# Heads of a score unit in three spare PSUM banks, held work released at once, and loads one stage ahead, in a planned transformer block

## The chip, the cores and the metric

The kernel runs on one core of a Trainium2 chip. The metric is device time in microseconds (us), the median of several executions of the whole program. A program starts its five engines side by side; each works through its own instructions in order, and they meet at semaphores. PE is TensorE (matmuls; PEld its weight loads), DVE is VectorE, ACT is ScalarE, POOL is GpSimd, and SP here only issues DMAs, also in order.

## The reference

One transformer block with adaptive layer norm, in fp32: 8 sequences of 1024 tokens, width 512, 16 heads of 32, an MLP of width 2048.

```python
mod = silu(condition) @ Wada + bada
sh_a, sc_a, gt_a, sh_m, sc_m, gt_m = split(mod, 6, axis=1)
xm = layernorm(x, g1, be1) * (1 + sc_a) + sh_a
x = x + gt_a * attention(xm, Wqkv, Wproj, bproj)   # causal, softmax over keys
xm = layernorm(x, g2, be2) * (1 + sc_m) + sh_m
h = gelu(xm @ W1 + b1, approximate=False)
x = x + gt_m * (h @ W2 + b2)
```

`x` and the output are (8, 1024, 512), `condition` is (8, 512).

## The kernel before

**Blocks and two streams.** The kernel treats 16 blocks n = 0..15, two halves of 512 tokens for each of 8 sequences; `h` is 0 for a first half, 1 for a second. Two streams share PE. The *attention stream* (`attend`, L1392) goes over the blocks and in each over 4 groups of 4 heads. The *linear stream* (`linear`, L1069) is a generator that goes through a list of steps by window, `plan[w]` (L228 to L264): `k`, `q`, `v` projections, `at` and `mt` (transposes of the normalized input for attention and for the MLP), `proj` (output projection, L844), `u` (four up projections, L865), `d` (four parts of the down projection, L914), and the loads and gate rows that they need. While attention works on block n, the linear stream does the output projection and MLP of block n-1 and the projections of later blocks. The last window, `plan[NB]`, has no attention beside it.

**The planner.** Nothing of the order is decided on the chip. While the program is written, the kernel keeps its own estimate of when each engine is free (`now`) and when each buffer is written or read for the last time (`written`, `left`; L104 `due`). A value that is not yet even issued has the time `NEVER`, infinity. The linear stream yields what its next matmul needs; `wait_of` (L1092) makes a waiting time of it, and `linear_wait` (L1103) is the smallest over the main linear thread and its side threads (transposes, and the last two products of a Strassen projection, run as side threads). Before each piece of attention, `step_aside` (L1135) fills PE with linear matmuls as long as the attention piece would wait longer than the linear one, or as long as the linear stream is behind its pace (`stream["due"]`, raised by `pace`). If `linear_wait` is `NEVER`, the loop breaks at once and attention is issued, wait or no wait.

**Attention by units.** A *score unit* (`scores`, L1196) makes scores of 128 queries by up to 512 keys for the 4 heads of a group into the PSUM tile `sc`, 4 banks (L1208); DVE adds the causal mask on diagonal units (L1220) and takes the row maxima (L1228). A *weight unit* (`weights_T`, L1282) makes the transposed scores `st` in the same 4 banks (L1294, maxima subtracted by L1305), ACT exponentiates them into `pT` (L1317), POOL zeroes what lies above the diagonal (L1322) and adds the units of a group for the row sums (L1429). `weigh` (L1334) multiplies with v into `po` (L1345). `finish` (L1355) sums over partitions (L1363), ACT copies, DVE inverts in four pieces (L1378), POOL multiplies (L1383); after the fourth group of a block this sets `attended`, for which `proj` of that block waits. The PSUM tile `st`/`sc` has one buffer: the next unit's matmuls wait until DVE or ACT has read it. Three further banks (`banks`, L163) belong to the linear stream and to the small sums of `finish` and `maxima_rows` (L1260). The eighth bank is `po`.

The score units of a group are issued during the group ahead of it. In `attend` each weight unit is a slot k of n_slots, and `upto` (L1406 to L1408) says how many score units of the next group are to be issued by the end of that slot. A block with h = 0 has 3 weight and 3 score units a group, one with h = 1 has 7 of each.

**Held work.** DVE work that can wait (statistics, inversions) is put in `jobs` and issued when DVE is not ahead of PE in the plan (L500). ACT work that changes the function table (the square root of a layer norm, `root` L551; the normalization `apply` L558; `gelu` L868) is put in `excursions`; `run_excursions(1)` issues one after each weight unit (L1417) and, in blocks with h = 0, one after each score unit (L1436). `work` (L1106) issues everything held when the linear stream has nothing to do, but `step_aside` does not call it then.

**Preparation.** The Strassen sums of the weights W1 and W2 are made once, in 8 stages of 4 sums (`preparation`, L670): four loads by SP, 12 us of planned waiting, four sums by `either` (L148: DVE or POOL, whichever is free by its rule), each stored to DRAM by SP. It advances only when POOL or DVE is not ahead of PE in the plan (L694). The first up projection issues all that is left before it goes on (L883).

**Weights.** `fetch` (L321) loads weight pieces through a ring of 9 buffers on SP, in the order in which the plan will use them (`order`, L310).

Of the kernel before, what the change touches and what calls it, by code (L numbers as in the profile page):

```python
# [22 lines left out]
def kernel(  # L23
# [33 lines left out]
    nc = tc.nc  # L57
# [167 lines left out]
    def mlp_steps(n):  # L225
# [7 lines left out]
        + [("mod", 3), ("at", 2), ("v", 1), ("mod", 4), ("k", 2), ("gates", "m"), ("columns_m",)],  # L233
    }
    late = []
    for w in range(1, NB):
        n = w - 1
        m = mlp_steps(n)
        even = blocks[n][1] == 0
        rows_a = [("rows", blocks[n][0], "a")] if even else []  # L240
        rows_m = [("rows", blocks[n][0], "m")] if even else []
        own = m[:1] + ([("load_xa", w + 2)] if w + 2 < NB else []) + m[1:3]
        own += [("norm_a", w + 2)] if w + 2 < NB else []
        if w == NB - 1:
            steps = late + [("load_xr", n)] + rows_a + [("proj", n), ("v", w)]
            steps += [("mt", n)] + rows_m + own + m[3:6]
            late = m[6:]
        else:

            steps = late + [("v", w), ("load_xr", n)] + rows_a + [("proj", n), ("k", w + 1)]  # L250
            if w == 1:
                steps = [("load_xr", n)] + rows_a + [("proj", n)]
            steps += [("mt", n), ("q", w + 1)] + rows_m + own
            at = [("at", w + 2)] if w + 2 < NB else []
            if blocks[w][1] == 0:

                steps += m[3:5]
                late = m[5:6] + at + m[6:]
            else:
                steps += m[3:6] + at  # L260
                late = m[6:]
        plan[w] = steps
    n = NB - 1
    plan[NB] = [("load_xr", n), late[0], ("proj", n), late[1], ("mt", n)] + mlp_steps(n)  # L264
# [21 lines left out]
    def pieces_of(step):  # L286
# [4 lines left out]
        if kind == "gates":  # L291
            return [(Wada, GATES[step[1]][0], kh, fh) for kh, fh in RAW]
        if kind == "proj":
            return [(Wproj, 0, k) for k in range(NC)]
# [224 lines left out]
    def excursion(job, first=False):  # L519
        if alone[0]:  # L520
            job()
        else:
            excursions.insert(0 if first else len(excursions), job)

    def run_excursions(limit=None):
        n = len(excursions) if limit is None else min(limit, len(excursions))
        for _ in range(n):
            excursions.pop(0)()
# [4 lines left out]
    def normalize(tiles, key, sources):  # L533
# [8 lines left out]
        def statistics(t):  # L542
            st = small.tile([P, nc.vector.BN_STATS_DIM], F32, tag="st", name=f"st_{key}_{t}")
            nc.vector.bn_stats(st, tiles[t])
            nc.vector.bn_aggr(mv[:, t, :], st)
            note("DVE", 850, [sources[t]], [("mv", key)])
            if t == NTT - 1:
                excursion(root)
                excursion(apply)
# [120 lines left out]
    def preparation():  # L670

        for w in (W1, W2):
            for i in range(NQ):
                stage = act.tile([P, NC, TB], F32, tag="hT", name=f"prep_{LABEL[id(w)]}_{i}", bufs=NQ)
                got = {}
                for j, kf in enumerate(RAW):
                    a = next(a for a in ("A11", "A12", "A21", "A22") if FULL[a] == kf)
                    got[a] = stage[:, j, :]
                    nc.sync.dma_start(
                        got[a].rearrange("p (k n) -> p k n", n=HB), quarter(w, i, *kf)  # L680
                    )
                ready = now["PE"] + 12000
                for out, a, b, op, name in IN_PLACE:
                    yield ready
                    keys = [("prep", w is W2, i, a), ("prep", w is W2, i, b)]
                    either(got[out], got[a], got[b], op, keys, [("prep", w is W2, i, out)])
                    keep(w, i, name, got[out])
# [3 lines left out]
    def run_preparation(everything=False):  # L691
        while prepared[0] is not None:
# [4 lines left out]
            try:  # L697
                prepared[0][1] = next(prepared[0][0])
            except StopIteration:
                prepared[0] = None  # L700

# [163 lines left out]
    def up(step):  # L865
# [11 lines left out]
        def finished():  # L877
            if q == NQ - 1:
                written["m used", n] = 0.0
            excursion(gelu, first=True)  # L880

        if (n, q) == (0, 0):
            run_preparation(True)  # L883
# [128 lines left out]
    def perform(step):  # L1012
# [28 lines left out]
        elif kind == "at":  # L1041
            n = step[1]
            guards = [("m used", n - 3)] if n > 2 else [("v done", 0)] if n == 2 else []
            start(modulated(f"a{n}", *columns_of["a"], blocks[n][0], guards))
        elif kind == "sums":
# [12 lines left out]
        elif kind == "preps":  # L1058
            prepared[0] = [preparation(), 0.0]
        elif kind == "rows":  # L1060
# [45 lines left out]
    def work():  # L1106

        if linear_wait() == NEVER:
            run_jobs(True)
            run_excursions()  # L1110
        assert linear_wait() < NEVER
# [23 lines left out]
    def step_aside(reads, writes):  # L1135


        while threads():
            own, other = wait_of((reads, writes)), linear_wait()
# [56 lines left out]
    def scores(n, g, parts):  # L1196
# [5 lines left out]
        reads = [("qT", n), ("kT", n - h + parts[0][1])]  # L1202
        step_aside(reads, ["st"])
# [28 lines left out]
        if units[unit_at[0] + 1 :] == [] or units[unit_at[0] + 1][:2] != (n, g):  # L1232
            split_maxima(n, g, h)
# [158 lines left out]
    def attend():  # L1392
        previous = None
        for n in range(NB):
# [5 lines left out]
            for g in range(NC):  # L1400
                nxt = groups.index((n, g)) + 1
                for k in range(n_slots):
                    upto = len(units)
                    if nxt < len(groups):
                        lo, m = first_unit[groups[nxt]], len(score_units(*groups[nxt]))
                        upto = lo + min(m, -(-(k + 2) * m // n_slots))  # L1406
                        if k == n_slots - 1 and nxt + 1 < len(groups):
# [6 lines left out]
            for g, k, upto in slots:  # L1414
# [16 lines left out]
                previous = (n, g, parts, pT, slot, k == n_slots - 1)  # L1431
                while unit_at[0] < upto:
# [4 lines left out]
                    pace(ns)  # L1437
        return previous
# [104 lines left out]
```

## Time and profile before

| what | value |
|---|---|
| median of 3 executions | 3678.65 us (3678.53 to 3679.02) |
| the profiled execution | 3678.31 us, of which the span of instructions is 3676.6 us |
| mean granted TensorE clock | 0.993 |
| DVE busy | 2158.9 us, 59% |
| ACT busy | 1327.8 us, 36% |
| POOL busy | 2044.1 us, 56% |
| DMA | 430.34 MB, a mean of 117 GB/s |
| PE busy in 300 to 400 us / 1000 to 1100 / 2800 to 2900 | 99.63 / 99.99 / 99.99 us of 100 |
| PE busy in 100 to 200 / 200 to 300 / 3300 to 3400 / 3500 to 3600 | 84.04 / 88.87 / 88.83 / 90.70 us of 100 |

The share of PE is an average over stages. In most of the span PE is busy without a break; the four stretches in the last row are where it is not. A stretch is best read by the idle time in front of single PE instructions, which the timeline names with the instruction that ended it. Busy time of PE also grows where the granted clock is lower, with no more work done.

### The profile page before, as it was taken

The page shows a single profiled execution, that of the slowest core. Times are in us where ns is not written, and L with a number is a line of the kernel's source. Part 1 is how long each engine was busy: PE and PEld are TensorE (multiplying, and loading weights), DVE is VectorE, ACT ScalarE, POOL GpSimd, SP SyncE. Part 2 cuts the span into 40 slices and gives each one's busy share as a digit, 9 for nine tenths or more (in the row PEclk, how much of TensorE's full clock was granted, in tenths as well). Part 3 has the DMA queues.
Part 4 walks back from the last instruction along what each step waited for, and adds up shares of the span by engine and source line. Part 5 has one row for each costly group of instructions (what it writes and reads, how often), then busy time and mean ns, then how long its engine had stood idle before and what let it go on. Part 6 is the DMA issues. An engine that isn't in the chain of part 4 may idle for free.

```text
span 3676.6 us, 121132 instructions
## 1 busy us (share of the span) xinstructions
PE 3575.4 (97%) x54821; PEld 1767.9 (48%) x54821; DVE 2158.9 (59%) x2447; ACT 1327.8 (36%) x1412; POOL 2044.1 (56%) x2064
## 2 busy tenths in 40 slices
PE   8889999999999999999999999999999999998989
PEld 4424445445554455544445454444544445454445
DVE  5756675564746557465565666646666465654542
ACT  2334334252333523335242452424425144341421
POOL 3576645656455663566536665356653556444661
PEclk9989999999999999999999999999999999999999
DMA  6633333433333343433434333343333433333334
GB/s 208 195 118 99 119 94 107 126 103 122 112 110 118 105 125 111 139 96 97 125 108 136 97 98 119 113 132 101 102 119 111 134 104 113 105 106 122 89 111 133
DMA packets 307893, 430.34 MB, mean 117 GB/s; under 512 B 25900, under 2 KB 176236, under 8 KB 307380
## 3 DMA queue, kind: packets, MB, share of 16 engines
q1 hardware_dynamic: 307264, 422.56, 38.1%
q8 instruction: 432, 7.08, 0.8%
q14 instruction: 81, 0.66, 0.1%
q10 hardware_dynamic: 116, 0.03, 0.0%
HBM read 394.12 MB, written 28.38 MB: 115 GB/s over the span
## 4 chain that ended last, share of the span: by engine, by line
PE 86%; DVE 7%; ACT 2%; POOL 2%; issue 2%; DMA 0%; SPq 0%; ACTq 0%; POOLq 0%; DVEq 0%
PE bank L199 58%; PE st L1294 8%; PE sc L1208 8%; PE po L1345 7%; DVE mx L1228 2%; PE st L1305 2%; PE bank L1363 2%; POOL pT L1429 1%; PE bank L606 1%; ACT pT L1317 1%; DVE hT L929 1%; DVE sc L1220 1%; DVE xr L156 1%; DVE t_m L156 1%; PE bank L1268 0%
## 5 line engine op out<-in xcount | busy, mean ns | idle before, releaser
L1429 POOL TENSOR_TENSOR pT<-pT,pT 128x512 f32<-128x512 f32 (+3 forms) x1280 | 1207.8, 979 | 548.7 <-ACT pT L1317 382.4
L1317 ACT ACTIVATE pT<-st 128x2048 f32<-128x2048 f32 (+1 forms) x320 | 546.4, 1708 | 1020.1 <-PE st L1305 972.5
L199 PE MATMUL bank<-w,hT 128*32 128x256 f32 x14336 | 808.7, 380 | 4.9 <-DVE hT L929 2.1
L1228 DVE TENSOR_REDUCE mx<-sc 128x4 f32<-128x2048 f32 (+3 forms) x384 | 668.9, 1756 | 205.4 <-PE sc L1208 198.7
L199 PEld LDWEIGHTS bank<-w,hT 128*32 128x32 f32 x14336 | 453.2, 110 | 357.8 <-issue 61.3
L199 PE MATMUL bank<-xm_m,w 128*32 128x256 f32 x8192 | 506.5, 380 | 0.5 <-DVE u_u L191 0.5
L1322 POOL TENSOR_SCALAR_AFFINE_SELECT pT<-pT 128x512 f32<-128x512 f32 x256 | 177.8, 706 | 576.2 <-ACT pT L1317 575.9
L199 PE MATMUL bank<-t_m,w 128*32 128x256 f32 x6144 | 383.1, 380 | 2.4 <-DVE t_m L625 1.0
L1294 PE MATMUL st<-qT,kT 32*128 32x512 f32 (+3 forms) x3072 | 343.0, 531 | 37.1 <-DVE mx L1228 35.8
L199 PEld LDWEIGHTS bank<-xm_m,w 128*32 128x32 f32 x8192 | 254.3, 110 | 248.9 <-issue 95.8
L1208 PE MATMUL sc<-kT,qT 32*128 32x512 f32 (+3 forms) x3072 | 340.2, 527 | 10.5 <-DVE mx L1228 5.8
L1345 PE MATMUL po<-pT,v 128*32 128x512 f32 (+3 forms) x3072 | 315.6, 498 | 6.5 <-POOL pT L1322 6.5
L1220 DVE TENSOR_TENSOR sc<-sc,mask 128x512 f32<-128x512 f32 (+1 forms) x192 | 167.9, 875 | 251.2 <-PE sc L1208 223.0
L199 PEld LDWEIGHTS bank<-t_m,w 128*32 128x32 f32 x6144 | 193.0, 110 | 174.3 <-issue 50.2
L199 PE MATMUL bank<-w,qT 128*32 128x512 f32 x2048 | 243.1, 602 | 6.1 <-POOL qT L1383 3.2
L199 PE MATMUL bank<-xm_a,w 128*32 128x256 f32 x3968 | 243.1, 381 | 0.0
L1378 DVE RECIPROCAL rec<-rec 128x128 f32<-128x128 f32 x256 | 223.6, 917 | 21.0 <-ACT rec L1369 21.0
L1294 PEld LDWEIGHTS st<-qT,kT 32*128 32x128 f32 x3072 | 129.5, 185 | 202.0 <-issue 60.7
L1208 PEld LDWEIGHTS sc<-kT,qT 32*128 32x128 f32 x3072 | 126.8, 184 | 175.0 <-ACT pT L1317 84.7
L191 DVE TENSOR_TENSOR hT<-bank,u_u 128x512 f32<-128x512 f32 x192 | 130.3, 686 | 120.4 <-PE bank L199 118.4
L199 PE MATMUL bank<-t_a,w 128*32 128x256 f32 x2944 | 186.6, 382 | 0.0
L1317 ACT ACT_TABLE_LOAD x88 | 112.9, 1283 | 183.2 <-PE st L1305 182.5
(184 smaller groups left out, 3552.9 us busy)
## 6 DMA issues: line engine op xcount, KB each, us to landing
w<-in_L_cond_W_dram SPq DMA_DIRECT2D x384, 256.0 KB, 2.9
w<-kept_up_S SPq DMA_DIRECT2D x256, 256.0 KB, 2.6
w<-kept_down_S SPq DMA_DIRECT2D x256, 256.0 KB, 2.7
w<-kept_qkv_S SPq DMA_DIRECT2D x180, 256.0 KB, 2.9
w<-in_L_cond_Wqkv_dram SPq DMA_DIRECT2D x147, 256.0 KB, 3.5
hat<-in_x_dram SPq DMA_DIRECT2D x64, 256.0 KB, 3.5
w<-in_L_cond_Wproj_dram SPq DMA_DIRECT2D x64, 256.0 KB, 3.5
xr<-in_x_dram SPq DMA_DIRECT2D x64, 256.0 KB, 4.5
```

The source lines that it names most:

```text
L156: nc.vector.tensor_tensor(out, a, b, op)
L191: nc.vector.tensor_tensor(out, src, other, op)
L199: nc.tensor.matmul(ps[r, :], lhsT[:, r], rhs, start=start, stop=stop, skip_group_check=True)
L1208: nc.tensor.matmul(sc[:, j, c0 : c0 + w], qTs[n][r, g, ts(qt, P)], keys_of(n, kh)[r, g, :w], start=True, stop=True, skip_group_check=True,)
L1220: nc.vector.tensor_tensor(diagonal, diagonal, mask[:, :span].unsqueeze(1).to_broadcast([P, HPG, span]), ALU.add,)
L1228: nc.vector.tensor_reduce(mx[:, kh, qt, :], sc[:, :, c0 : c0 + w], axis=AX.X, op=ALU.max)
L1294: nc.tensor.matmul(st[:, j, c0 : c0 + w], kT[r, g, ts(k % NTT, P)], qT[r, g, TB - w :], start=(c0 == 0), stop=False, skip_group_check=True,)
L1317: nc.scalar.activation(pT[:, :, :used], st[:, :, :used], AF.Exp, scale=scale)
L1322: nc.gpsimd.affine_select(diagonal, diagonal, pattern=[[0, HPG], [1, P]], compare_op=ALU.is_ge, fill=0.0, base=0, channel_multiplier=-1,)
L1345: nc.tensor.matmul(po[r, TB - w :], v[:, k % NTT, g * P + j * hd : g * P + (j + 1) * hd], pT[:, j, c0 : c0 + w], start=(k == 0), stop=last ...
L1378: nc.vector.reciprocal(some, some)
L1429: nc.gpsimd.tensor_tensor(into, into, pT[:, j, c0 : c0 + w], ALU.add)
```

## The change

The change has six parts.

1. In `attend`, for the last group of block 0 (n, g) = (0, 3), no score units of the next group are asked for in slot 0 and one in slot 1 (counted from the group's first, so that the two units issued earlier already cover it). In its last slot one score unit is issued, then the last weight unit is weighed and finished at once (`close`), then come the other score units and the rows of maxima.
2. `scores` takes one of two ways. If the linear stream would wait over 3 us, none of the three banks is live, and the 4-bank tile would be free over 1 us later than a bank, the unit is made by `scores_by_heads`: three heads in the three banks, then the fourth, with a mask and a reduction for each head. Otherwise it is made as before.
3. `hurry` issues held jobs and excursions whose inputs are due within 500 ns, whenever `step_aside` finds that the linear stream has nothing to do. Excursions now carry what they wait for.
4. `preparation` loads one stage ahead; the first up projection waits for a mark, `prepared`, in place of issuing the rest.
5. The order of steps: `columns_m` before the third `k` projection in window 0; in window 15, `proj` and `mt` of block 14 go ahead of parts 2 and 3 of the down projection of block 13 and of the last `v`; in the last window, part 3 of the down projection of block 14 runs as a side thread (`beside`), beside the main thread that waits for block 15's attention.
6. `work` finishes the preparation when nothing else is left.

```diff
-        + [("mod", 3), ("at", 2), ("v", 1), ("mod", 4), ("k", 2), ("gates", "m"), ("columns_m",)],
+        + [("mod", 3), ("at", 2), ("v", 1), ("mod", 4), ("columns_m",), ("k", 2), ("gates", "m")],
...
         if w == NB - 1:
-            steps = late + [("load_xr", n)] + rows_a + [("proj", n), ("v", w)]
-            steps += [("mt", n)] + rows_m + own + m[3:6]
+            steps = late[:1] + [("load_xr", n)] + rows_a + [("proj", n), ("mt", n)] + late[1:]
+            steps += [("v", w)] + rows_m + own + m[3:6]
...
-    plan[NB] = [("load_xr", n), late[0], ("proj", n), late[1], ("mt", n)] + mlp_steps(n)
+    plan[NB] = [("load_xr", n), late[0], ("beside", late[1]), ("proj", n), ("mt", n)] + mlp_steps(n)
...
+    def hurry():
+
+        while jobs and due(jobs[0][1]) <= now["PE"] + 500:
+            jobs.pop(0)[0]()
+        while excursions and due(excursions[0][1]) <= now["PE"] + 500:
+            excursions.pop(0)[0]()
...
     def preparation():
...
+        load(*todo.pop(0))
+        while loaded:
+            if todo:
+                load(*todo.pop(0))
+            w, i, got, ready = loaded.pop(0)
+            for out, a, b, op, name in IN_PLACE:
+                yield ready
+                keys = [("prep", w is W2, i, a), ("prep", w is W2, i, b)]
+                either(got[out], got[a], got[b], op, keys, [("prep", w is W2, i, out)])
+                keep(w, i, name, got[out])
...
         if (n, q) == (0, 0):
-            run_preparation(True)
+            yield ["prepared"], []
...
+        elif kind == "beside":
+            start(perform(step[1]))
...
         if linear_wait() == NEVER:
             run_jobs(True)
             run_excursions()
+        if linear_wait() == NEVER:
+            run_preparation(True)
...
         while threads():
+            if linear_wait() == NEVER:
+                hurry()
...
+        if (
+            linear_wait() > 3000
+            and not any(live)
+            and wait_of((reads, ["st"])) > wait_of((reads, [BANK])) + 1000
+        ):
+            scores_by_heads(n, g, parts, mx, reads)
+        else:
+            scores_at_once(n, g, parts, mx, reads)
...
+    def scores_by_heads(n, g, parts, mx, reads):
+
+        h = blocks[n][1]
+        for some in (range(HPG - 1), range(HPG - 1, HPG)):
+            step_aside(reads, [BANK])
+            of = {j: lin_bank() for j in some}
+            for qt, kh, c0, w in parts:
+                for j, bank in of.items():
+                    r = slice(j * hd, (j + 1) * hd)
+                    nc.tensor.matmul(
+                        banks[bank][:, c0 : c0 + w],
+                        qTs[n][r, g, ts(qt, P)],
+                        keys_of(n, kh)[r, g, :w],
...
+            for j, bank in of.items():
+                if parts[0][1] == h:
+                    first, span = parts[0][3] - P, len(parts) * P
+                    diagonal = banks[bank][:, first : first + span]
+                    nc.vector.tensor_tensor(diagonal, diagonal, mask[:, :span], ALU.add)
...
+                for qt, kh, c0, w in parts:
+                    nc.vector.tensor_reduce(
+                        mx[:, kh, qt, j : j + 1], banks[bank][:, c0 : c0 + w], axis=AX.X, op=ALU.max
+                    )
...
+                live[bank] = False
...
+                        if (n, g) == (0, NC - 1) and k < n_slots - 1:
+                            upto = lo + k
...
+                if (n, g, k) == (0, NC - 1, n_slots - 1):
+
+                    next_scores()
+                    close(*previous)
+                    previous = None
...
+                if previous is None:
+                    maxima_rows()
```

More of the change, by code (lines that the diff above doesn't have):

```diff
@@ L292, in pieces_of @@
             return [(Wada, GATES[step[1]][0], kh, fh) for kh, fh in RAW]
+        if kind == "beside":
+            return pieces_of(step[1])
         if kind == "proj":
@@ L517, with excursion @@
     alone = [True]
-    def excursion(job, first=False):
+    def excursion(job, reads, first=False):
         if alone[0]:
@@ L522, in excursion @@
         else:
-            excursions.insert(0 if first else len(excursions), job)
+            excursions.insert(0 if first else len(excursions), (job, reads))
     def run_excursions(limit=None):
@@ L527, in run_excursions @@
         for _ in range(n):
[L528 removed]
+            excursions.pop(0)[0]()
[3 more added lines that the diff above has]
+        while excursions and due(excursions[0][1]) <= now["PE"] + 500:
+            excursions.pop(0)[0]()
     hats = {}
@@ L547, in statistics @@
             if t == NTT - 1:
-                excursion(root)
-                excursion(apply)
+                excursion(root, [("mv", key)])
+                excursion(apply, [("rstd", key)])
         def root():
@@ L670, in preparation, with load @@
     def preparation():
[L672 to L687, printed above, removed]
+        todo = [(w, i) for w in (W1, W2) for i in range(NQ)]
+        loaded = []
+        def load(w, i):
+            stage = act.tile([P, NC, TB], F32, tag="hT", name=f"prep_{LABEL[id(w)]}_{i}", bufs=NQ)
+            got = {}
+            for j, kf in enumerate(RAW):
+                a = next(a for a in ("A11", "A12", "A21", "A22") if FULL[a] == kf)
+                got[a] = stage[:, j, :]
+                nc.sync.dma_start(got[a].rearrange("p (k n) -> p k n", n=HB), quarter(w, i, *kf))
+            loaded.append((w, i, got, now["PE"] + 12000))
+        load(*todo.pop(0))
[8 more added lines that the diff above has]
+                keep(w, i, name, got[out])
     prepared = [None]
@@ L700, in run_preparation @@
                 prepared[0] = None
+                written["prepared"] = 0.0
     summed = {}
@@ L879, in finished @@
                 written["m used", n] = 0.0
-            excursion(gelu, first=True)
+            excursion(gelu, [("h", n, q)], first=True)
         if (n, q) == (0, 0):
-            run_preparation(True)
+            yield ["prepared"], []
         written["g", n, q] = NEVER
@@ L1059, in perform @@
             prepared[0] = [preparation(), 0.0]
+            written["prepared"] = NEVER
         elif kind == "rows":
@@ L1202, in scores, with scores_at_once @@
         reads = [("qT", n), ("kT", n - h + parts[0][1])]
+        if (
[6 more added lines that the diff above has]
+            scores_at_once(n, g, parts, mx, reads)
+        if units[unit_at[0] + 1 :] == [] or units[unit_at[0] + 1][:2] != (n, g):
+            split_maxima(n, g, h)
+    def scores_by_heads(n, g, parts, mx, reads):
[10 more added lines that the diff above has]
+                        keys_of(n, kh)[r, g, :w],
+                        start=True,
+                        stop=True,
+                        skip_group_check=True,
+                    )
+                note_pe(2 * COLUMN * w, "rows", reads, [("l", bank) for bank in of.values()])
+            for j, bank in of.items():
[3 more added lines that the diff above has]
+                    nc.vector.tensor_tensor(diagonal, diagonal, mask[:, :span], ALU.add)
+                    note("DVE", 120 + 1.04 * span, [("l", bank)])
+                for qt, kh, c0, w in parts:
+                    nc.vector.tensor_reduce(
+                        mx[:, kh, qt, j : j + 1], banks[bank][:, c0 : c0 + w], axis=AX.X, op=ALU.max
+                    )
+                    note("DVE", 170 + w, [("l", bank)], [("mx", n, g)])
+                live[bank] = False
+    def scores_at_once(n, g, parts, mx, reads):
+        h = blocks[n][1]
         step_aside(reads, ["st"])
@@ L1231, in scores @@
             note("DVE", 170 + 4.14 * w, ["st"], [("mx", n, g)])
-        if units[unit_at[0] + 1 :] == [] or units[unit_at[0] + 1][:2] != (n, g):
-            split_maxima(n, g, h)
     def split_maxima(n, g, h):
```

## The prediction

> **What bounds the kernel now.** The page first: PE is busy nearly all the span, and the chain that ended last is PE's.
>
> ```profile
> PE 3575.4 (97%) x54821; PEld 1767.9 (48%) x54821; DVE 2158.9 (59%) x2447; ACT 1327.8 (36%) x1412; POOL 2044.1 (56%) x2064
> ...
> PE 86%; DVE 7%; ACT 2%; POOL 2%; issue 2%; DMA 0%; SPq 0%; ACTq 0%; POOLq 0%; DVEq 0%
> ```
>
> So a change that leaves PE's work alone can only win what PE stands idle or runs at a low clock. Cutting the span into windows of 100 us and then 25 us puts most of that into four stretches; between them PE is busy 98 to 100%. The windows' columns are stretch, its length, busy time of PE, PEld, DVE, ACT, POOL, granted clock, DMA share, GB/s:
>
> ```profile
> 171.60:211.50 39.90, 22.53 (x158) 6.53 (x154) 20.77 (x21) 8.31 (x7) 27.76 (x31) 0.70 0.50 170
> 252.70:280.30 27.60, 20.19 (x123) 5.73 (x117) 14.66 (x16) 14.26 (x15) 13.36 (x12) 0.81 0.07 23
> 3332.00:3386.00 54.00, 43.41 (x502) 16.77 (x492) 22.41 (x31) 14.20 (x17) 21.86 (x26) 0.94 0.39 123
> 3530.00:3556.00 26.00, 19.92 (x160) 5.84 (x156) 11.34 (x14) 2.36 (x3) 14.32 (x15) 0.93 0.10 34
> ```
>
> Busy time at clock 0.70 flatters. I price the instructions of each stretch at their dense intervals (pieces of the chain): 8 score matmuls of 512 columns 1.07 us, 8 of `po`, L1363 or `proj` 0.86, 4 of L1305 0.22, 16 transposes 2.1, 32 of 256 columns 1.73, smaller units in proportion. That makes 14.3, 14.1, 39.2 and 15.9 us of work, so **lost**: A 25.6, B 13.5, C 14.8, D 10.1, together 64.0 us. PE's timeline says what ended the idle time of A:
>
> ```profile
> 175.54 0.71 PE L1208 MATMUL sc<-kT,qT 32*128 32x256 f32 x8 [3.37 <-DVE mx L1228]
> 180.99 1.24 PE L1294 MATMUL st<-qT,kT 32*128 32x256 f32 x8 [4.73 <-DVE mx L1228]
> ...
> 189.95 1.42 PE L1208 MATMUL sc<-kT,qT 32*128 32x512 f32 x8 [2.42 <-DVE mx L1228]
> 193.76 2.09 PE L1294 MATMUL st<-qT,kT 32*128 32x512 f32 x8 [2.39 <-DVE mx L1228]
> ```
>
> No linear matmul stands between them: the list of window 0 has ended, and `proj` of block 0 waits for block 0's last group, which is itself spread between score units of block 1, each holding the one `sc`/`st` tile for a matmul and a DVE reduction. The clock matters too. The Trainium skill ("TensorE: Matmul & The Clock Gate", HAM oscillation) allows idle gaps up to about 3.4 us before the clock halves; by that rule most gaps here would cost themselves alone, and A would be worth its idle 17.4 us. The windows disagree: after one idle gap of 2.85 us at 3342 the next two 2 us windows have clock 0.65 and 0.50, then 1.00, and A has 0.70 throughout. I take 25.6.
>
> In B `proj` is done and everything waits for the normalization of block 0's MLP input. Its square root and its application are held, one released per weight unit, 9 us apart:
>
> ```profile
> 262.62 1.28 ACT L552 ACT_TABLE_LOAD   x1
> 263.92 0.30 ACT L552 ACTIVATE rstd_m<-mv_m,eps 128x4 f32<-128x4 f32 x1
> 264.23 1.28 ACT L1317 ACT_TABLE_LOAD   x1
> 269.99 1.88 ACT L1317 ACTIVATE pT<-st 128x2048 f32<-128x2048 f32 x1 [4.48 <-PE st L1305]
> 271.77 2.92 ACT L569 ACTIVATE xh_m<-xr,offset_m,rstd_m 128x512 f32<-128x512 f32 x4
> ```
>
> **The order of block 0's last group (A).** I follow it from 153.9, the end of `finish` for group (0,2). The three weight units need no score unit between them now: exponentials of 1.88, 1.88 and 1.02 us end at 154.5, 158.0 and 160.0 (matmuls 1.3 and 0.8 between). POOL then has 1.2 us of select, 6.0 of additions (4 x 1.05 + 4 x 0.46), 0.6 and 2.8: 168.6. L1363 0.86, copy 0.58, four inversions of 0.92 behind one 2.29 reduction, POOL's product 1.3: about 177.5, where `proj` had its attention at 208.3 and started at 211.5. In these 23.6 us PE has 144 + 16 linear matmuls left (7.8 + 3.4), 5.1 of attention and score units of block 1; DVE makes about four of those (4.2). Sum 20.5: 3 us stay lost, and one block of four preparation sums on POOL (4 x 1.27), likely there, makes it 5.5. **A gains 20** (bounds: 25.6 if nothing is lost; 10 if two blocks of sums and all score units come ahead).
>
> Part 2, by heads: once `proj` comes so early it has few places to act (the ends of A and B). A whole unit's reduction costs 4 x 680 against 2291 ns (+0.43 us) and a mask four smaller ones; no trace row has it running. Bound: minus 3 us where `sc` would have been waited for, plus 4 if DVE is late with ten such units. I take 0: A's sum already fills PE.
>
> **Held work at once (B).** The loop asks `hurry` whenever the linear stream has nothing. Statistics (4 x 0.85) then lie under `q` of block 2. From the moment of starving: table and root 1.6, two DVE operations 0.9, application 2.9, last transposes, copy and difference 2.1: 7.5 us, or 10 with an exponential (table 1.28, 1.88, counted once in part) between root and application, where it was 27.6. Attention fills it at B's density (14.1/27.6), so 4.5 us stay lost: **B gains 9** (4 to 13). The table loads were paid before, too.
>
> **Window 15 (C).** C begins with `proj` of block 14 waiting for gate rows: SP issues them at 3339.0, behind the stores of block 13's down projection, which wait for POOL until 3335.1. That is 2.85 us of idle time and 1.3 of low clock. Then `v` runs until 3361.9, and only then are root and application released, one per weight unit. Moved ahead, the loads of block 14 pass those stores on SP, and `d` 2 and 3 (6.9 + 13.8 us on PE) and `v` (12.1) cover adds, statistics and gate rows. The `y` buffers are fewer: one holds `v3` between parts 1 and 2, so each `y` of `proj` waits for the add of the one ahead (0.69 + 1.28 us); a tile takes PE 3.45, so nothing. After `v` about 10 us remain as in B, 4 of them lost. **C gains 11** (7 to 13).
>
> **Part 3 beside (D).** From 3530 on PE waits for POOL and the quotient; `d` 3 (13.8 us) stands ready and fills it. But it is what covers block 15's normalization now:
>
> ```profile
> 3543.14 12.75 PE L199 MATMUL bank<-w,qT 128*32 128x512 f32 x104 [3.25 <-POOL qT L1383]
> 3555.72 13.99 PE L199 MATMUL bank<-w,hT 128*32 128x256 f32 x256
> 3569.64 1.55 PE L606 MATMUL bank<-ident,xh_m 128*128 128x128 f32 x12
> ```
>
> The last hat lands at 3563.6, 7.9 us behind `proj`'s end. Side threads win ties, so `d` 3 goes first: `proj` ends near 3559.8, the last hat comes at 3567.7, `u` starts at about 3570 cold (8 us of idle, some 1.8 us of half clock): 10.1 won, 9.7 paid. **D: 0** (minus 8 if `d` 3 is used up before PE idles, plus 4).
>
> **Edits with one answer.** `columns_m` (2.2 us of DVE) leaves a place where the next mask waited for it, and lies under `k` at 142: in A's sum. Preparation a stage ahead moves some 16 sums (20 us, mostly POOL) from 181 to 251 to earlier, where POOL is 58% busy; its four loads and four stores per stage also stand earlier on SP, in front of weight pieces. No L199 waits for a weight piece of these stages, with 9 buffers ahead (9 x 1.73 us even back to back): nothing, and 5 us at most. The steady 3000 us have the same instructions: plus or minus 2.
>
> **Sum.** 20 + 9 + 11 + 0 = 40 us off the profiled execution (3678.31 us; span 3676.6, 1.7 outside it; the median is 3678.65): **3638 us**.
>
> **The rivals.** (a) POOL binds block 0's end: preparation sums come in twice ahead of its additions, PE's queue stands at L1363 with the score units behind it; A gives 10: 3648. For it: POOL is the busiest engine in A (27.76 of 39.9). Against: A's POOL time includes additions of block 1. (b) The end gives back: `d` 3 is used up early, or POOL, which carries the chain from 3496 to 3535, holds block 15's last group where it is, so C's gain is waited for again: 11 lost, 3649. Against: POOL has 74 of 113 us busy from 3387 to 3500. (c) `hurry` seldom acts, because what is held is not yet due within 500 ns at the calls there are; B gains 2, C 4: 3652. (d) **Slower**: the first `u` now waits for the last preparation sum, which may only go when POOL or DVE is idle in the plan. Before, 28 sums took from 75.8 to 219.4, 5.1 us each; 32 at that pace end at 240, about when `u` wants to start (178 plus the 69 us from `proj` to `u` now, less some 10). Denser attention could stretch it; each us beyond has attention alone and loses 0.64 (25.6/39.9). From 302 on the 40 us are gone; at 320 it is 3689. Against: the 12 us of waiting in each stage now overlap.
>
> **Chances.** Forecast 0.55 (own range 3626 to 3645), (a) 0.14, (b) 0.13, (c) 0.10, (d) 0.08. The range of 8 in 10 takes in (a) to (c) and the far ends of A to C: 3620 to 3660. A measurement here tells 0.2%, 7.4 us, from no change. (d) is slower nearly always, 0.07; same 0.04, from (b) with (c) together and mild (d); faster 0.89.
>
> **What would show it.** `proj` of block 0 starting near 178 without a gap like 4.73 ahead of it; root and application of block 0 a few us apart, `u` between 230 and 250; no wait for gate rows in window 15 and its transposes right behind `v`; at the end `d` 3 ahead of `proj`, then 7 to 8 us idle before the transposes. I would be wrong if preparation sums stand on POOL in front of block 0's L1429, if the first `u` waits for a sum, or if the saturated middle grows by over 5 us.

## The result, and the profile after

| what | before | after |
|---|---|---|
| median of 5 executions | 3678.65 us (3678.16 to 3680.71) | 3665.73 us (3662.55 to 3667.84) |
| ratio | | 0.9963, 95% interval 0.9951 to 0.9974 |
| the profiled execution, its span | 3678.31, 3676.6 us | 3667.59, 3665.9 us |

Faster by 13 us, a third of the forecast 40, and outside the range. The page after, its engines and the shares of the chain that ended last:

```profile
PE 3578.9 (98%) x54821; PEld 1770.8 (48%) x54821; DVE 2157.1 (59%) x2466; ACT 1328.1 (36%) x1410; POOL 2039.3 (56%) x2060
...
PE 87%; DVE 7%; POOL 2%; ACT 2%; issue 2%; DMA 0%; SPq 0%; ACTq 0%; POOLq 0%; DVEq 0%
```

PE still bounds the span. The stretches of the prediction after the change (the first two at the old limits, the other two where their work now lies; same columns):

```profile
171.60:211.50 39.90, 30.53 (x188) 10.07 (x190) 31.47 (x37) 5.41 (x5) 22.06 (x20) 0.74 0.52 172
252.70:280.30 27.60, 27.04 (x334) 11.40 (x333) 17.17 (x17) 12.09 (x12) 14.29 (x12) 1.00 0.30 84
3299.00:3356.00 57.00, 55.43 (x823) 28.18 (x815) 24.53 (x35) 8.57 (x11) 33.27 (x33) 0.97 0.55 170
3500.00:3561.00 61.00, 45.17 (x500) 20.46 (x492) 24.26 (x31) 12.90 (x14) 38.77 (x36) 0.87 0.23 70
```

B and C are nearly full, as forecast. A still idles 9 us at a low clock, and D idles 16 us, more than before (9 in the same limits). The times of the same work say what that was worth. I read from PE's timeline when `finish` of group (0,0) starts, and when `proj` starts for blocks 1 and 13:

```
                                      before    after   difference
first finish (start-up)                 99.1    100.5      +1.4
first finish to proj of block 1        355.0    345.2      -9.8
proj of block 1 to proj of block 13   2678.8   2675.6      -3.2
proj of block 13 to the span's end     543.6    544.6      +1.0
```

A and B together, forecast at 29, brought 10, and C and D, forecast at 11, nothing. The start-up has no part in it: over all the profiles of this study the first `finish` lay between 97.2 and 102.5 us, and between 97.2 and 100.5 in kernels with the same code up to there, so single profiles are compared from that mark on.

**A.** `proj` of block 0 was forecast at 177.5. PE's timeline after:

```profile
184.21 1.00 PE L1247 MATMUL bank<-kT,qT 32*128 32x384 f32 x1 [5.04 <-DVE mx L1263]
...
199.72 3.64 PE L199 MATMUL bank<-w,qT 128*32 128x512 f32 x16
```

`finish` of block 0 came some 4 us behind the forecast, 1.4 of them start-up: its matmuls end at 173.7 (169.5 in the sum) and ACT's copy at 174.6 (170.0). The rest of the delay follows. DVE's timeline shows the four inversions, and POOL's the quotient:

```profile
179.17 0.93 DVE L1444 RECIPROCAL rec<-rec 128x128 f32<-128x128 f32 x1
180.04 0.66 DVE L1288 TENSOR_TENSOR sc<-sc,mask 128x512 f32<-128x512 f32 x1
180.73 2.29 DVE L1296 TENSOR_REDUCE mx<-sc 128x4 f32<-128x2048 f32 x1
...
186.33 0.94 DVE L1444 RECIPROCAL rec<-rec 128x128 f32<-128x128 f32 x1
...
192.17 0.94 DVE L1444 RECIPROCAL rec<-rec 128x128 f32<-128x128 f32 x1
...
197.13 0.94 DVE L1444 RECIPROCAL rec<-rec 128x128 f32<-128x128 f32 x1
```

```profile
198.25 1.49 POOL L1449 TENSOR_TENSOR qT<-top,rec 128x512 f32<-128x512 f32 x1 [3.98 <-DVE rec L1444]
```

From the copy to the quotient it takes 23.7 us, where the sum had 6.0. Reductions stand between the inversions: the code of `hurry` issues the first because its input is due; the second depends on the first, is not due until that has run in the plan, and is left for a later call. Meanwhile a score unit and its reductions are issued, and DVE works in order.

**The end.** After the change `d` 3 ends at 3520.8. PE's timeline from there (the L1429 pieces left out):

```profile
3520.17 0.61 PE L199 MATMUL bank<-w,hT 128*32 128x256 f32 x8
3526.68 1.08 PE L1411 MATMUL po<-pT,v 128*32 128x256 f32 x8 [5.90 <-POOL pT L1388]
...
3537.28 13.06 PE L199 MATMUL bank<-w,qT 128*32 128x512 f32 x104 [3.09 <-POOL qT L1449]
3555.99 0.47 PE L615 MATMUL bank<-ident,xh_m 128*128 128x128 f32 x1 [5.66 <-ACT xh_m L578]
```

The filler was gone before the first of three waits. The quotient of block 15 came 5.9 us earlier than before (3537.28 against 3543.14), though the first `u` of block 14 had started 29.6 us earlier (3356.39 against 3385.98): the linear stream moved, the attention stream much less.

### The profile page after: what moved, and what is told of

It reads as the page before. It is cut to its first block, busy times and chain, and to the rows that moved or that the text cites. A ratio compares the mean times of both kernels' runs of the same rounds, so it can differ in the third digit from the quotient of the medians.

```text
span 3665.9 us, 121141 instructions
## 1 busy us (share of the span) xinstructions
PE 3578.9 (98%) x54821; PEld 1770.8 (48%) x54821; DVE 2157.1 (59%) x2466; ACT 1328.1 (36%) x1410; POOL 2039.3 (56%) x2060
## 4 chain that ended last, share of the span: by engine, by line
PE 87%; DVE 7%; POOL 2%; ACT 2%; issue 2%; DMA 0%; SPq 0%; ACTq 0%; POOLq 0%; DVEq 0%
PE bank L199 59%; PE st L1360 8%; PE sc L1276 8%; PE po L1411 7%; DVE mx L1296 2%; PE st L1371 2%; PE bank L1429 2%; POOL pT L1497 2%; PE bank L615 1%; DVE hT L946 1%; DVE sc L1288 1%; DVE xr L156 1%; ACT pT L1383 1%; DVE t_m L156 1%; PE bank L1334 0%
## 5 line engine op out<-in xcount | busy, mean ns | idle before, releaser
L199 PE MATMUL bank<-w,hT 128*32 128x256 f32 x14336 | 808.9, 380 | 2.8 <-DVE hT L946 2.1
L1296 DVE TENSOR_REDUCE mx<-sc 128x4 f32<-128x1024 f32 (+3 forms) x381 | 664.3, 1757 | 192.0 <-PE sc L1276 185.4
L199 PEld LDWEIGHTS bank<-w,hT 128*32 128x32 f32 x14336 | 452.0, 110 | 355.5 <-issue 58.9
L199 PE MATMUL bank<-xm_m,w 128*32 128x256 f32 x8192 | 507.1, 381 | 0.6 <-ACT rec L1435 0.5
L199 PE MATMUL bank<-t_m,w 128*32 128x256 f32 x6144 | 383.2, 380 | 0.9 <-ACT hT L186 0.9
L199 PEld LDWEIGHTS bank<-xm_m,w 128*32 128x32 f32 x8192 | 253.3, 110 | 252.5 <-issue 98.7
L1276 PE MATMUL sc<-kT,qT 32*128 32x256 f32 (+3 forms) x3048 | 340.0, 527 | 2.9 <-DVE mx L1296 1.9
L1288 DVE TENSOR_TENSOR sc<-sc,mask 128x1024 f32<-128x1024 f32 (+1 forms) x191 | 166.7, 873 | 250.2 <-PE sc L1276 227.1
L199 PEld LDWEIGHTS bank<-t_m,w 128*32 128x32 f32 x6144 | 191.8, 110 | 175.7 <-issue 54.2
L199 PE MATMUL bank<-w,qT 128*32 128x512 f32 x2048 | 244.5, 604 | 3.1 <-POOL qT L1449 3.1
L199 PE MATMUL bank<-xm_a,w 128*32 128x256 f32 x3968 | 244.2, 382 | 0.0
L199 PE MATMUL bank<-t_a,w 128*32 128x256 f32 x2944 | 187.2, 382 | 0.0
```

The lines of the kernel that those rows point to most:

```text
L199: nc.tensor.matmul(ps[r, :], lhsT[:, r], rhs, start=start, stop=stop, skip_group_check=True)
L1276: nc.tensor.matmul(sc[:, j, c0 : c0 + w], qTs[n][r, g, ts(qt, P)], keys_of(n, kh)[r, g, :w], start=True, stop=True, skip_group_check=True,)
L1288: nc.vector.tensor_tensor(diagonal, diagonal, mask[:, :span].unsqueeze(1).to_broadcast([P, HPG, span]), ALU.add,)
L1296: nc.vector.tensor_reduce(mx[:, kh, qt, :], sc[:, :, c0 : c0 + w], axis=AX.X, op=ALU.max)
```

## The experiments

Times are medians of a kernel, ratios are to the kernel before on the same chip. "Proj 1" is the time from the first `finish` to `proj` of block 1 in the profile: 355.0 before, 345.2 after, and 345.5 to 346.7 in three profiles whose code is the same up to there.

**1. Block 0's inversions at once.**

```diff
                     close(*previous)
+                    run_jobs(True)
                     previous = None
```

> The changed kernel, with the four inversions and the quotient of block 0's last group issued right behind its sum. In the changed kernel the inversions stand at 179.2, 186.3, 192.2 and 197.1 us, one between two reductions of score units each, and the quotient at 198.3, so proj of block 0 starts at 199.7. Theory I (the held inversions are what A's forecast missed: each is released only when the plan sees the one before it done): inversions together by 182, quotient by 184, proj before 187, 500-us marks some 8 us earlier, 3657 us. Rival H (the score units by heads load DVE and the banks): inversions together but proj not before 193, under 3 us gained. Rival P (preparation sums hold DVE and POOL): the same, quotient on POOL behind sums.

Measured 3671.82 us, 0.9977 (0.9969 to 0.9986). The mechanism of theory I is there, DVE's timeline:

```profile
172.32 3.39 DVE L1444 RECIPROCAL rec<-rec 128x128 f32<-128x128 f32 x4 [1.14 <-ACT rec L1435]
```

`proj` of block 0 starts at 172.4, earlier than I had forecast. And the kernel is not faster: proj 1 is 352.6, 7 us behind the changed kernel. Windows of this kernel show where the time went:

```profile
200.00:388.00 188.00, 186.07 (x2800) 89.66 (x2792) 128.73 (x134) 80.13 (x79) 127.27 (x112) 1.00 0.36 113
388.00:437.00 49.00, 32.99 (x268) 11.34 (x264) 22.05 (x34) 16.32 (x13) 37.55 (x41) 0.79 0.06 17
```

The idle time is not gone, it moved. Up to 388 PE is full; then no linear matmul stands on PE until 437.8, and attention is alone, at clock 0.79, with a DMA share of 0.06. What comes next on the list is `v` of block 2, which may not overwrite its buffer before block 1's attention is over. All three theories had the size wrong, mine too.

One more thing differs from the changed kernel. With linear work at hand in A, the condition for units by heads no longer holds there. The first matmuls by heads are these, on PE's timeline:

```profile
400.74 1.14 PE L1247 MATMUL bank<-kT,qT 32*128 32x384 f32 x12
```

So this kernel has the inversions at once and none of A's units by heads, and its loss against the changed kernel can't be put down to the inversions alone. The fair partner is the next experiment, which has none either; there `proj` of block 0 starts 24 us later behind the first `finish` (97.8 against 73.7), and proj 1 only 3.7 us later.

**2. No units by heads.**

```diff
-            linear_wait() > 3000
+            False
             and not any(live)
```

> The changed kernel without score units by heads (all at once in the three-bank tile). Three such units run in it, all from 178 to 194 us. Theory I: the inversions stay apart, proj of block 0 starts after 195, total 3663 to 3670 (the two ways share waiting for the same DVE). Rival H: proj starts 8 us earlier or more, total 3658 or less. If the units by heads earn something: proj later than 202, total 3669 or more.

Measured 3677.49 us, 0.9993 (0.9984 to 1.0001); proj 1 is 356.3. `proj` of block 0 starts as early as in the changed kernel (97.8 against 99.2 us behind the first finish), so rival H falls, and the total is that of the third expectation, with another reason. In this kernel's PE timeline the units wait for each other's reduction in the one tile:

```profile
180.30 2.09 PE L1276 MATMUL sc<-kT,qT 32*128 32x384 f32 x16 [4.87 <-DVE mx L1296]
186.21 1.24 PE L1276 MATMUL sc<-kT,qT 32*128 32x256 f32 x8 [3.83 <-DVE mx L1296]
189.61 2.09 PE L1276 MATMUL sc<-kT,qT 32*128 32x512 f32 x8 [2.16 <-DVE mx L1296]
```

By heads the next unit's matmuls go into the idle banks and need not wait for the tile. The changed kernel makes two units of A so (24 matmuls at L1247; the expectation above counts three). Without them block 1's last `finish` comes 16 us later (340.3 behind the first one against 324.4), and the linear stream stands still for 24 us ahead of `v` of block 2 (417.6 to 441.5). Without the part that I priced at 0, 11 to 12 of the 13 us are gone.

**3. The preparation as before.** (`preparation` and its use in `up` taken back.)

> The changed kernel with the preparation as before: one stage of sums at a time, loaded when the one ahead is done, and forced out at the first u. Rival P: PE's marks around 146 us come back by the 2.4 us that the changed kernel is late there, proj of block 0 starts 8 us earlier, total 3659 or less. Theory I: up to 2.4 us come back at 146, proj still after 192; the sums that are left at the first u stand in its way and cost 5 to 10 us there, total 3668 to 3675.

Measured 3677.23 us, 0.9992 (0.9983 to 1.0001); proj 1 is 358.0. `proj` of block 0 did not move (97.3), so rival P falls. The first `u` is where it costs, as theory I said but dearer; DVE's and then PE's timeline of this kernel:

```profile
245.47 1.42 DVE L156 TENSOR_TENSOR prep_down<-prep_down 128x512 f32<-128x512 f32 x2 [9.17 <-DMA prep_down<-in_L_cond_W_dram]
```

```profile
248.91 1.24 PE L1353 MATMUL st<-qT,kT 32*128 32x256 f32 x8 [7.26 <-DVE mx L1289]
```

The planner comes to the first `u`, issues the sums that are left, and DVE stands 9.2 us in front of one whose load has not landed, with a score unit's mask and reduction behind it. Before the change the first `u` came at 280.3, 29 us behind the last sum. So the other parts pay only with the look-ahead. That it would win nothing without them follows from this slack and was not run.

**4. `d` 3 behind `proj` of block 15.**

```diff
-    plan[NB] = [..., late[0], ("beside", late[1]), ("proj", n), ("mt", n)] + mlp_steps(n)
+    plan[NB] = [..., late[0], ("proj", n), late[1], ("mt", n)] + mlp_steps(n)
```

> The changed kernel with d 3 of block 14 back behind proj of block 15. Theory E (block 15's last group is bound by POOL and by when its units are let in, d 3 only fills): PE idles 14 us more ahead of proj, proj ends where it does (3550), d 3 then covers the 5.7 us before the transposes, first u some 3 us later: 3668 to 3670. Rival: d 3's gain and loss cancel, within 1 us of the changed kernel (3665 to 3667); or d 3 behind proj is better, under 3663.

Measured 3664.99 us, 0.9963 (0.995 to 0.9975): the rival's "cancel". The place of `d` 3 is worth nothing here, as the sum's term D had it.

**5. The old order of block 0's last group.** (The edits to `upto` and the early `close` taken back.)

> The changed kernel with the old order of block 0's last group (score units of block 1 between its weight units again). Theory K (from block 0 on, the attention stream through the one sc/st tile sets when block 1 is attended, and the linear stream has to wait for that before v of block 2 anyhow; what the changed kernel won there came from score units by heads, which use the idle banks): proj of block 0 starts near 205 to 212, yet proj of block 1 within 4 us of the changed kernel's (446), total 3662 to 3670. Theory of the forecast (the order of the last group wins what PE idles): proj of block 1 near 454, total 3673 or more.

Measured 3664.4 us, 0.9959 (0.9947 to 0.9972), the time of the changed kernel. `proj` of block 0 starts 103.0 us behind the first finish against 99.2, and proj 1 is 339.9, earlier than with the new order. The part to which I gave 20 us is worth none. It moves six score units of block 1 from before `finish` to behind it; the attention stream has to make them anyway. About half of what proj 1 wins with the old order is lost again behind it: from `proj` of block 1 to `proj` of block 13 the five profiles with the old order take 2678.0 to 2680.1 us, the nine with the new one 2675.1 to 2676.7.

**6. POOL relieved in block 15's last group.**

```diff
+                            if (n, g) == (NB - 1, NC - 1) and j % 2:
+                                nc.vector.tensor_tensor(into, into, pT[:, j, c0 : c0 + w], ALU.add)
...
+                                continue
                             nc.gpsimd.tensor_tensor(into, into, pT[:, j, c0 : c0 + w], ALU.add)
```

> The changed kernel with every second addition of exponentials of block 15's last group on DVE in place of POOL. POOL is busy 37.2 of 40 us from 3490 to 3530. If POOL binds the end (rival b): quotient of block 15 6 to 9 us earlier, the idle gap of 5.9 us before the last po gone, total 3658 to 3661. If the end is late because block 15's attention came late as a whole and POOL only happens to be full: under 2 us, 3664 or more.

Measured 3657.68 us, 0.9938 (0.9925 to 0.9952). POOL does bind the end of the changed kernel: the gap of 5.90 in front of the last `po` is 0.71, that of 3.09 in front of `proj` 0.64, and 2.80 stand between. PE's timeline here:

```profile
3521.54 2.60 PE L1429 MATMUL bank<-pT,ones 128*32 128x512 f32 x8 [2.80 <-POOL pT L1501]
...
3529.77 11.37 PE L199 MATMUL bank<-w,qT 128*32 128x512 f32 x104 [0.64 <-POOL qT L1449]
```

**7. `v` of block 15 a window earlier.** Why was block 15's attention so late that POOL had to make its last group in one piece? PE's timeline of the changed kernel:

```profile
3281.38 0.40 PE L1371 MATMUL st<-mrow,minus_ones 32*128 32x384 bf16 x8
3281.70 17.47 PE L199 MATMUL bank<-w,hT 128*32 128x256 f32 x320
3298.99 13.92 PE L199 MATMUL bank<-w,qT 128*32 128x512 f32 x128
3312.73 20.90 PE L199 MATMUL bank<-w,hT 128*32 128x256 f32 x384
...
3345.53 1.04 PE L1411 MATMUL po<-pT,v 128*32 128x512 f32 x8
```

For 64 us no attention stands on PE. `weigh` of block 15's own half needs `v` of block 15, which stands last among these steps; it can't go between the parts of `d`, which keep partial sums in the buffers that `v` uses. It can go into window 14:

```diff
-            steps += [("mt", n), ("q", w + 1)] + rows_m + own
+            steps += [("mt", n), ("q", w + 1)] + ([("v", w + 1)] if w == NB - 2 else [])
+            steps += rows_m + own
...
-            steps += [("v", w)] + rows_m + own + m[3:6]
+            steps += rows_m + own + m[3:6]
```

The run also has experiment 4's edit, which alone is worth nothing.

> The changed kernel with v of block 15 taken into window 14, behind q of block 15, and d 3 of block 14 behind proj of block 15 as before. In the changed kernel block 15's attention stands still while 37 linear groups (64 us) run up to the end of v. Theory V (the end is late because of that hold, not because of POOL or of the place of d 3): attention of block 15 ends with some 14 linear groups unspent, so d covers the wait for the quotient and d 3 the wait for the hats; PE idles under 5 us from 3400 to 3600 (17.7 in the changed kernel), total 3650 to 3655. Rival b (POOL binds whatever the order): under 5 us gained, 3661 or more.

Measured 3639.04 us, 0.9891 (0.9877 to 0.9904): 27 us faster than the change. Block 15's last `finish` comes at 3478.4, 49 us earlier, and PE's timeline has no gap over 1.21 us left there:

```profile
3475.34 0.64 PE L1412 MATMUL po<-pT,v 128*32 128x256 f32 x8 [1.21 <-POOL pT L1389]
...
3479.24 23.92 PE L199 MATMUL bank<-w,hT 128*32 128x256 f32 x440
3502.98 13.92 PE L199 MATMUL bank<-w,qT 128*32 128x512 f32 x128
3516.72 14.00 PE L199 MATMUL bank<-w,hT 128*32 128x256 f32 x256
3530.64 2.19 PE L616 MATMUL bank<-ident,xh_m 128*128 128x128 f32 x16
```

**8. By heads also beside linear work.** (`linear_wait() > 3000` becomes `(linear_wait() > 3000 or n <= 2)`, with experiment 1's edit.)

> The changed kernel with block 0's inversions at once and with score units by heads also where the linear stream has work, for blocks 0 to 2, whenever the three banks are free. With inversions at once alone the linear stream ran dry from 388 to 437 us. Theory K: the attention stream gets ahead in the banks, the dry stretch shrinks, idle time of PE from 100 to 450 falls from 26 us to under 18, proj of block 1 before 446, total 3656 to 3663. Rival H (reductions by heads cost DVE more than they win): 3672 or more.

Measured 3680.27 us, 1.0 (0.9992 to 1.0009), proj 1 is 354.4: a miss. Against experiment 1, idle time of PE between the first finish and proj 1 falls from 26.8 to 22.4 us, but PE's busy time grows from 325.9 to 332.0, and the first finish itself comes 3.8 us later (102.5 against 98.7). No unit goes by heads in A here either; they stand at 50 to 57, 217 to 250 and 401 to 409 us. Beside linear work units by heads won nothing; why they cost this much there was not taken apart. The inversions at once together with A's units by heads were not run.

**9 and 10. Experiment 7 with experiment 5, and with 6 as well.**

> The changed kernel with v of block 15 in window 14 and d 3 of block 14 behind proj of block 15 (3639 us alone), and with the old order of block 0's last group as well (there proj of block 1 came 5.5 us earlier, counted from the first finish). If the two are independent: proj of block 1 340 us behind the first finish, PE idle under 4 us from 3300 to 3600, total 3633 to 3636. If the gain at the start is only spread of the attention stream that later blocks take back: 3639.

> The kernel before this one, with every second addition of block 15's last group on DVE too. POOL bound the end only where block 15's attention was late: with the linear work spread behind it, nothing is left to win, within 1.5 us of the kernel before this one. If POOL still binds: 3 us or more faster than it.

Measured 3639.06 us, 0.9887 (0.9873 to 0.99), and 3640.88 us, 0.9893 (0.988 to 0.9907). The old order in block 0 adds nothing, so what proj 1 gains with it (5 us in experiment 5, 2 to 3 in these two: 343.9 and 344.4 for 346.7) is not shown in the time. POOL's relief adds nothing either: with `v` early nothing is seen of POOL's limit.

**11. `v` early in the kernel before.** (The first half of experiment 7's edit, and `("v", w)` taken from the old list of window 15.)

> The kernel before the change with v of block 15 in window 14 and nothing else. Theory V: the hold of block 15's attention until v was there before the change too; its end is worth 20 us and more, less what the held root and application of block 14 cost (released one per weight unit, with the linear stream empty meanwhile: some 6 to 10 us): 3655 to 3668. If the order of window 15 in the change was needed for it: under 8 us gained, 3671 or more.

Measured 3673.69 us, 0.9983 (0.9974 to 0.9992). The gain is 6, as expected for the case that the change's order of window 15 is needed. The hats (normalized inputs) of block 14 are held, and PE has attention alone, with gaps, from 3386 to 3423. From its timeline:

```profile
3398.18 1.14 PE L1295 MATMUL st<-qT,kT 32*128 32x512 f32 x8 [2.41 <-DVE mx L1229]
...
3415.31 2.09 PE L1295 MATMUL st<-qT,kT 32*128 32x512 f32 x8 [4.18 <-DVE mx L1229]
...
3423.17 3.19 PE L607 MATMUL bank<-ident,xh_m 128*128 128x128 f32 x13
```

So the early `v` needs something of the change: 6 us alone, 13 us for the change alone, 41 together. The order of window 15 and `hurry`, which free the hats, are the likely parts; they were not run alone.

**12. Without `hurry`.** (The call in `step_aside` taken out.)

> The changed kernel without issuing held work when the linear stream is empty. Theory K (the linear stream has slack until v of block 2): the first u some 20 us later (near 180 us behind the first finish), but proj of block 1 within 6 us of the changed kernel's 345; window 15 loses 3 to 5; total 3666 to 3674. Theory of the forecast (what PE idles there is lost, B 9 and C 4): 3677 to 3681.

Measured 3670.68 us, 0.9973 (0.9963 to 0.9984). The first `u` is 19 us later (177.6 behind the first finish, 158.3 with `hurry`), the total some 4 us (the intervals overlap), in theory K's range (proj 1 a little outside its 6 us); of B's 9 and C's 4 less than half. Proj 1 is 351.5, 6 us later; 3 of these are lost already at the second finish (30 us behind the first, 27 in the changed kernel), and why is open. From the last matmul of `q` 2 to the first `u` 25.5 us pass, 12.9 in the changed kernel and 27.4 in the kernel before: here `hurry` does what it was made for.

## Why the prediction was wrong

**The step that failed is A's path to `proj` of block 0; behind it, "lost" was read as "can be won".** From the first `finish` to `proj` of block 1 each kernel in this table issues the same 4744 matmuls, 296.5 us of work at the dense intervals of the prediction (small ones in proportion). What a stretch takes beyond its work is lost. This is an estimate in us, by time behind the first `finish`; A is 70 to 113 and B 113 to 182 in the kernel before:

```
                            0 to 70   to 113   to 182   to proj 1    sum
before                          6.1     27.3     15.8         9.3   58.5
after                           6.5     22.1      8.4        11.7   48.7
1, inversions at once           6.4     13.6      4.0        32.1   56.1
2, no units by heads            6.2     21.3      9.0        23.2   59.8
3, old preparation              6.2     19.6     22.8        12.8   61.5
5, old order                    7.4     16.8      8.2        11.1   43.4
12, without hurry               8.7     23.3     13.4         9.6   55.0
```

A brought 5 in place of 20, B 7 of its 9, and 3 were lost elsewhere.

**A, plus 20, term "four inversions of 0.92 behind one 2.29 reduction".** They took 23.7 us in place of 6.0, the quotient came at 198.25 in place of 176, and until then PE had score units waiting for DVE. Experiment 1 shows that the mis-sized term is not all: against the kernel before it wins 14 us in A and loses 23 behind 182. Against experiment 2, which has no units by heads in A either, it loses 13 less up to 182 and 9 more behind. There the linear stream comes to `v` of block 2 before block 1 is attended, and it stands still for 50 us. A's sum followed the linear stream to `proj` of block 0 and no further. In the changed kernel this barrier does not bind; the last matmuls of `d` 3 and the first of `v` follow one another, though block 1's last `finish` was at 424.96:

```profile
432.33 1.50 PE L199 MATMUL bank<-w,hT 128*32 128x256 f32 x24
433.65 1.91 PE L199 MATMUL bank<-w,xm_a 128*32 128x256 f32 x32
```

The new order by itself is worth nothing (experiment 5).

**By heads, 0.** Without them 11 to 12 us are lost. I reasoned "once `proj` comes so early it has few places to act"; but it came late, and two units in A were enough. The table says where they count: not in A, where the loss is the same without them (21.3 and 22.1), but behind 182 (23.2 and 11.7). They let block 1's attention get ahead, where it used to wait for one tile, and so the barrier does not bind.

**Preparation, minus 0 to 5.** With the old one in its place 12 us are lost; the table has them in the stretch of B (22.8 for 8.4). What each part is worth does not add up: by heads and the preparation each cost nearly the whole gain when they are left out. Rival (d) had the right place, sums in front of the first `u`, but the wrong kernel: the look-ahead is what avoids it.

**B, plus 9.** From `proj` of block 0 to the first `u` 68.8 us became 59.1. ACT's timeline after the change has the root before `q` 2 has ended (at 245.9), and the application 7.5 us behind the root's table load, where it was 9.2:

```profile
242.69 1.28 ACT L561 ACT_TABLE_LOAD   x1
243.99 0.30 ACT L561 ACTIVATE rstd_m<-mv_m,eps 128x4 f32<-128x4 f32 x1
...
250.19 2.93 ACT L578 ACTIVATE xh_m<-xr,offset_m,rstd_m 128x512 f32<-128x512 f32 x4 [1.09 <-DVE offset_m L564]
```

The mechanism and its 9.7 us are as forecast, 7 of them by the table; the place, 258.8 for 230 to 250, follows from A.

**C, plus 11.** No wait for gate rows, transposes 2 us behind `v`: each step as forecast, and given back. The hold of block 15's attention ended 16.4 us earlier (3345.5 for 3361.9), 11.7 of which `proj` of block 13 was ahead already: C's reordering moved `u` of block 14 by 18 us more than that, and the attention stream by 5. The same estimate of lost time, behind `proj` of block 13:

```
                            to u of block 14   to the end of proj 15   rest    sum
before                                  23.3                    20.7    0.8   44.8
after                                   12.2                    24.2    9.3   45.7
4, d 3 behind proj                      10.7                    33.7    0.8   45.2
6, POOL relieved                        12.2                    15.7    8.7   36.6
7, v early, d 3 behind proj             12.1                     4.7    0.8   17.6
```

C's stretch wins its 11 us, and the wait for block 15's attention takes them back: 13 us more than before in experiment 4. **D, 0** is right in size and in mechanism: `d` 3 beside wins 9.5 us ahead of `proj` and pays 8.5 behind it (experiment 4 against the change; 10.1 and 9.7 in the sum).

What failed at the end is rival (b), which I gave 13%, with "C's gain is waited for again" and 11 us lost, measured 12 (C and D together plus 1.0 in place of minus 11). I had argued against it with POOL's 74 of 113 us from 3387 to 3500. That mean says nothing about the last 40 us, where POOL was full before the change too: 38.4 of 39 us from 3496 to 3535, and after it 37.2 of 40 from 3490 to 3530. And the reason that the last group fell there, a hold without attention on PE, stood in the trace of before: L199 alone from 3295.1 to 3361.9 us. Experiment 7 ends the hold, and the loss ahead of the end of `proj` falls from 24.2 to 4.7.

**The middle, plus or minus 2,** moved by 3.2, which goes with the new order in block 0 (experiment 5). Rivals (a) and (c) did not come: POOL stood idle for 10 us in A (180.4 to 190.5), and `hurry` acted.

**Left open.** What paces block 1's attention between 155 and 324 us behind the first finish, and so what would win the 21 us of idle time that are left before proj 1. A third buffer for `v`, which would lift the barrier, was not tried.

## What to carry to other kernels

Filling idle time of the busiest engine can be given back if the stream that fills it meets a barrier later: follow each stream to the next point where it must wait for the other, and compare the two streams' times there. When an experiment takes one fault away, check that the other parts of the change still act in it; experiment 1 switched one of them off. Look for long runs of one stream on the shared engine with none of the other, and for the one input that ends them; moving that input here was worth twice the whole change. When held work is issued "as soon as it is due", a chain of small steps is issued one at a time, with everything else between.

## What the runs showed of the hardware

In the end stretch idle time of PE cost over half as much again in clock. From `proj` of block 13 to the end of PE's work the changed kernel idles 20.8 us and experiment 7's kernel 3.6. The difference in time is 28.2 us; the other 11 are PE's busy time for the same matmuls, 516.5 against 505.5 us. Windows of the changed kernel and then of experiment 7's show it in the column before the last two:

```profile
3500.00:3566.00 66.00, 50.17 (x580) 23.10 (x576) 26.16 (x34) 14.37 (x16) 42.00 (x39) 0.87 0.23 69
```

```profile
3500.00:3566.00 66.00, 65.57 (x1064) 35.38 (x1060) 23.82 (x38) 14.31 (x21) 26.98 (x21) 1.00 0.51 158
```

The 104 matmuls of `proj` took 13.06 us behind the changed kernel's gaps of 5.90 and 3.09, and 11.37 in experiment 6 behind 2.80 and 0.64. The 0.70 that the prediction read for A of the kernel before "throughout" is a mean: windows of 5 us from 175 on read 0.50 to 0.93.
